# Row sums of attention over eight key blocks instead of four, with one add of each group on GpSimd

## The chip, the cores and the metric

The kernel runs on one core of one Trainium2 chip. The metric is the device time of one execution in microseconds (us); the median of several runs is given. The engines are TensorE (PE in the profile, its weight loads PEld), VectorE (DVE), ScalarE (ACT), GpSimd (POOL) and the queue of SyncE (SP).

## The reference, cut to what matters

The input is a batch of four images with 128 channels and 64 x 64 pixels. Layer 0 is group normalization, attention over the 4096 pixels of an image with four heads of 32 channels, an output projection and a residual. Layer 1 is two 3 x 3 convolutions with quantized weights, batch normalization, relu and a residual.

```python
x_norm = _group_norm(x, norm_w, norm_b)
qkv = jnp.einsum('oc,bchw->bohw', qkv_w, x_norm) + qkv_b[None, :, None, None]
q, k, v = jnp.split(qkv, 3, axis=1)
...
attn = jnp.einsum('bhid,bhjd->bhij', q, k) * scale
attn = jax.nn.softmax(attn, axis=-1)
out = jnp.einsum('bhij,bhjd->bhid', attn, v)
out = out.transpose(0, 1, 3, 2).reshape(b, c, h, w)
out = jnp.einsum('oc,bchw->bohw', proj_w, out) + proj_b[None, :, None, None]
return x + out
...
out = conv3x3_decomposed(x, lsq_quantize(w1, alpha1))
out = jax.nn.relu(batchnorm(out, gamma1, beta1))
out = conv3x3_decomposed(out, lsq_quantize(w2, alpha2))
out = batchnorm(out, gamma2, beta2)
out = jax.nn.relu(out + residual)
```

The change concerns the denominator of the softmax: for each head and query, the sum of the exponentials over all 4096 keys.

## The kernel before, in words

Attention is cut into 32 **blocks**: four images times eight groups of 512 queries. Each block goes through 32 **steps** (`kt`), one for each 128 keys. The keys lie on the partitions and the queries along the free dimension, so that the probabilities of one step are one tile `pt` of 128 partitions by four heads by 512 queries in float32 (128x2048). There are four such tiles (`bufs=4`).

A step consists of:

- `exp_step`: TensorE forms the scores of the four heads (L279) in two PSUM tiles `s` of two heads each, and ScalarE takes the exponential of each (L282). The pool of `s` has three tiles. The tiles of the projections and of the group norm's averages come from the same pool, in turn.
- `second`, which runs one step behind: `av_step` multiplies v with the probabilities and accumulates in `acc` (L289); `sum_step` adds probability tiles on VectorE (L302); `ones_step` (L306) multiplies the sum `r` with a matrix of ones on TensorE, which sums over the partitions and accumulates in `l`.
- `side_work`: the tasks of the block before, the quantization of the weights, the group norm of the next image (during the last but one block of an image) and its q, k and v projections (`project_qkv`, every fourth step of an image's last block, and of the very first block).

With `GROUPED = 4`, four steps share one product with ones: VectorE does three adds for four tiles. The product of a group is issued at the third step of the next group, behind `av_step`; that of a block's last group is a task of `finish`, `last_ones`, in the second step of the next block. The other tasks of `finish` follow, one per step: a copy of `l` to `ls` on ScalarE (L320), four reciprocals (L324), the running maxima `worst` and the product `at` (L327 to L329), an empty one, and `project`: the output projection `po` on TensorE (L333) and the residual add `xp` from PSUM on VectorE (L335).

Each engine works through its instructions in order. A scheduler sets that order from the order of the text and its own estimates. In the regular blocks it is that of the text but for small moves; in the first block the instructions of the weight quantization stand between others on VectorE. Semaphores follow from the tiles that an instruction reads and writes, and from the buffers that have to be free.

## Time and profile before

| | |
|---|---|
| median of 3 runs | 3028.28 us (3027.94 to 3031.02) |
| profiled execution | 3029.39 us, of it the span of the profile 3027.6 us |
| TensorE busy | 95% |
| VectorE busy | 73% |
| ScalarE busy | 69% |
| GpSimd busy | 1% |
| attention | ends at about 2699 us in the span, the convolutions follow |
| mean granted TensorE clock | 0.983 |

A line of the costliest groups reads: source line, engine, operation, tile written and tiles read, shapes of both (partitions x elements, type), count, then busy time and mean duration in ns, then the idle time of the engine just before these instructions and what ended most of it. A matrix product in float32 appears as two records. A line of the timeline reads: start in the span, duration, engine, line, operation, tiles, shapes, count of merged instructions, and in brackets the idle time before and what ended it. Busy time of TensorE counts pipelined products with modelled ends.

### The profile page before, as it was taken

Reading aid. Unit: us, or ns where it says so; the run is one execution under the profiler, and the core shown is the slowest. Engines: PE = TensorE matmul, PEld = TensorE weight load, DVE = VectorE, ACT = ScalarE, POOL = GpSimd, SP = SyncE. Lnnn points to the kernel's source line nnn. Section 1 sums busy time; section 2 is a strip of 40 time slices with the busy share of each in tenths; the row PEclk is TensorE's granted clock in tenths of the full one; section 3 lists DMA queues with packets and bytes.
Section 4 is the critical chain, followed back from the end, with each engine's and each line's share of the span. In section 5 each row is a group of like instructions: output and inputs, shape, how many; then the busy total and the mean of one; then the engine's idle time right before and its main releaser. Section 6 shows DMA issues by size and latency. Waiting matters only on the chain.

```text
span 3027.6 us, 45635 instructions
## 1 busy us (share of the span) xinstructions
PE 2884.3 (95%) x20050; PEld 928.2 (31%) x20050; DVE 2206.7 (73%) x1475; ACT 2100.7 (69%) x2209; POOL 18.5 (1%) x86
## 2 busy tenths in 40 slices
PE   5899999999999999999999999999999999989895
PEld 2222222223222222222222222232222222237773
DVE  8877777766777777767777777767777777763334
ACT  2488888856888888856888888757888888841223
POOL 1000000000000000000000000000000000000000
PEclk9899999999999999999999999999999999999997
DMA  6000000000000000000000000000000000000002
GB/s 124 9 1 1 1 1 1 1 1 1 1 1 1 1 1 1 1 1 1 1 1 1 1 1 1 1 1 1 1 1 1 1 1 1 1 1 1 1 0 113
DMA packets 36881, 21.30 MB, mean 7 GB/s; under 512 B 33777, under 2 KB 34545, under 8 KB 36673
## 3 DMA queue, kind: packets, MB, share of 16 engines
q1 hardware_dynamic: 32064, 16.91, 2.2%
q8 instruction: 159, 2.61, 0.4%
q10 hardware_dynamic: 4128, 1.05, 0.2%
q0 software_dynamic: 480, 0.33, 0.1%
q14 instruction: 50, 0.40, 0.0%
HBM read 9.90 MB, written 8.39 MB: 6 GB/s over the span
## 4 chain that ended last, share of the span: by engine, by line
PE 63%; DVE 28%; ACT 5%; issue 2%; DMA 1%; SPq 0%; DVEq 0%; POOL 0%; POOLq 0%; ACTq 0%
PE s L279 27%; PE acc L289 21%; DVE r L302 19%; PE ps L428 9%; PE l L306 5%; ACT p L282 5%; DVE rc L324 3%; DVE k L260 1%; DVE q L261 1%; DVE xp L335 1%; DVE at L329 1%; DVE worst L327 1%; DVE worst L328 1%; DMA out_dram<-y 0%; DVE st L222 0%
## 5 line engine op out<-in xcount | busy, mean ns | idle before, releaser
L282 ACT ACTIVATE p<-s 128x1024 f32<-128x1024 f32 x2048 | 1991.7, 1024 | 655.0 <-PE s L279 644.1
L279 PE MATMUL s<-q,k 32*128 32x512 f32 x8192 | 1293.6, 644 | 57.9 <-DVE q L261 47.0
L302 DVE TENSOR_TENSOR r<-r,p 128x2048 f32<-128x2048 f32 x512 | 1171.4, 2288 | 53.2 <-ACT p L282 9.2
L289 PE MATMUL acc<-p,v 128*32 128x512 f32 x8192 | 1100.9, 608 | 7.5 <-ACT av L313 7.5
L302 DVE TENSOR_TENSOR r<-p,p 128x2048 f32<-128x2048 f32 x256 | 586.7, 2292 | 541.8 <-ACT p L282 541.8
L279 PEld LDWEIGHTS s<-q,k 32*128 32x128 f32 x8192 | 411.5, 184 | 921.9 <-issue 548.5
L289 PEld LDWEIGHTS acc<-p,v 128*32 128x32 f32 x8192 | 162.1, 108 | 795.1 <-issue 761.7
L306 PE MATMUL l<-r,ones 128*32 128x512 f32 x2048 | 266.6, 592 | 1.8 <-DVE r L302 1.8
L459 ACT COPY cv<-ps 128x512 f32<-128x512 f32 x64 | 37.6, 588 | 208.3 <-PE ps L428 207.2
L428 PE MATMUL ps<-lo,wq 128*128 128x512 f32 x576 | 151.4, 408 | 11.6 <-DVE lo L419 11.6
L428 PE MATMUL ps<-hi,wq 128*128 128x512 f32 x576 | 148.4, 402 | 0.0
L428 PEld LDWEIGHTS ps<-lo,wq 128*128 128x128 f32 x576 | 110.4, 192 | 41.6 <-issue 12.1
L428 PEld LDWEIGHTS ps<-hi,wq 128*128 128x128 f32 x576 | 109.3, 190 | 29.4
L460 DVE BATCH_NORM_STATS2 st<-cv 128x6 f32<-128x512 f32 x64 | 44.3, 692 | 100.3 <-ACT cv L459 100.3
L306 PEld LDWEIGHTS l<-r,ones 128*32 128x32 f32 x2048 | 66.5, 110 | 155.3 <-issue 151.7
L324 DVE RECIPROCAL rc<-ls 128x128 f32<-128x128 f32 x128 | 108.2, 909 | 1.8 <-ACT ls L320 1.8
L478 ACT ACTIVATE t<-cv,bc,ba 128x1088 f32<-128x1088 f32 (+1 forms) x16 | 21.1, 1328 | 31.5 <-DVE lo L419 27.7
L418 DVE CAST hi<-t 128x1188 fp32r<-128x1188 f32 x16 | 12.5, 778 | 41.1 <-PE ps L428 39.7
L333 PE MATMUL po<-at,wp 128*128 128x512 f32 x64 | 36.9, 660 | 5.4 <-DVE at L329 5.4
L418 DVE CAST hi<-xp 128x1188 fp32r<-128x1188 f32 x16 | 12.3, 776 | 38.7 <-PE ps L428 38.7
L256 PE MATMUL pqk<-xn,wqkv 128*128 128x512 f32 x64 | 37.0, 660 | 3.0 <-DVE xn L253 3.0
L264 PEld LDWEIGHTS pv<-wqkv,xn 128*128 128x128 f32 x256 | 33.7, 192 | 15.6 <-issue 15.3
(98 smaller groups left out, 500.3 us busy)
## 6 DMA issues: line engine op xcount, KB each, us to landing
out_dram<-y SPq DMA_DIRECT2D x16, 512.0 KB, 2.7
xp<-in_x_dram SPq DMA_DIRECT2D x14, 512.0 KB, 7.7
wr<-in_L_conv_w_dram SPq DMA_DIRECT2D x6, 192.0 KB, 2.4
xp<-in_x_dram ACTq DMA_DIRECT2D x2, 512.0 KB, 10.5
wqkv<-in_L_conv_qkv_w_dram POOLq DMA_DIRECT2D x1, 192.0 KB, 6.6
bv<-in_L_conv_qkv_b_dram POOLq DMA_DIRECT2D x1, 64.0 KB, 7.2
wp<-in_L_conv_proj_w_dram POOLq DMA_DIRECT2D x1, 64.0 KB, 6.9
gamma<-in_L_conv_gamma_dram POOLq DMA_DIRECT2D x2, 0.5 KB, 6.5
```

What stands on the lines that cost most here:

```text
L256: nc.tensor.matmul(ps[:, 0, :], wqkv[:, P : 2 * P], xn, start=True, stop=True)
L264: nc.tensor.matmul(ps[:, 0, i * P : (i + 1) * P], xn[:, i * P : (i + 1) * P], wqkv[:, 2 * P : 3 * P], start=True, stop=True)
L279: nc.tensor.matmul(s[h // 2][:, h % 2, :], k[h * D : (h + 1) * D, c0 : c0 + P], q[h * D : (h + 1) * D, :], start=True, stop=True)
L282: nc.scalar.activation(pt[:, 2 * i : 2 * i + 2, :], s[i], AF.Exp, scale=SCALE)
L289: nc.tensor.matmul(acc[h * D : (h + 1) * D, :], v[:, kt % KB, h * D : (h + 1) * D], pt[:, h, :], start=(kt == 0), stop=(kt == NK - 1))
L302: nc.vector.tensor_tensor(r, pts[kt - 1] if n == 1 else r, pts[kt], ALU.add)
L306: nc.tensor.matmul(l[h * D : (h + 1) * D, :], ones, sums[g][:, h, :], start=(g == 0), stop=(g == NK // GROUPED - 1))
L324: nc.vector.reciprocal(rc[:, cs], ls[:, cs])
L333: nc.tensor.matmul(ps[:, 0, :], wp, at, start=True, stop=True)
L428: nc.tensor.matmul(ps, w[:, tap, :], part[:, j * RB + kh : j * RB + kh + RB, kw : kw + W], start=(n == 0), stop=(n == 2 * TAPS - 1))
L459: nc.scalar.copy(dst, ps)
L460: nc.vector.bn_stats(st[:, b * NB + j, :], dst)
```

## The change

`GROUPED` becomes 8, so that a block has four products with ones. The first two tiles of a group are added on GpSimd into a tile of their own, `rp` (one buffer). VectorE adds the third and fourth into `r` (one buffer instead of two), then one tile at each of the four following steps, and at the sixth step also `rp`.

```diff
-GROUPED = 4
+GROUPED = 8
...
         def sum_step(blk, kt, pts, sums):
-            n = kt % GROUPED
-            if n == 0:
-                return
+            n, g = kt % GROUPED, kt // GROUPED
             if n == 1:
-                sums[kt // GROUPED] = pex.tile([P, HEADS, FB], F32,
-                                               name=f"r_{blk[0]}_{blk[1]}_{kt}", tag="r")
-            r = sums[kt // GROUPED]
-            nc.vector.tensor_tensor(r, pts[kt - 1] if n == 1 else r, pts[kt], ALU.add)
+                sums["pool"] = pex.tile([P, HEADS, FB], F32, name=f"rp_{blk[0]}_{blk[1]}_{kt}",
+                                        tag="rp", bufs=1)
+                nc.gpsimd.tensor_tensor(sums["pool"], pts[kt - 1], pts[kt], ALU.add)
+            if n == 3:
+                sums[g] = pex.tile([P, HEADS, FB], F32, name=f"r_{blk[0]}_{blk[1]}_{kt}", tag="r",
+                                   bufs=1)
+                nc.vector.tensor_tensor(sums[g], pts[kt - 1], pts[kt], ALU.add)
+            if n > 3:
+                nc.vector.tensor_tensor(sums[g], sums[g], pts[kt], ALU.add)
+            if n == 5:
+                nc.vector.tensor_tensor(sums[g], sums[g], sums["pool"], ALU.add)
```

The condition in `second` that issues a product with ones (`kt % GROUPED == 2 and kt >= GROUPED`) is unchanged; with 8 it holds at steps 10, 18 and 26.

## The prediction

> **What bounds the kernel now.** I read the page's engine line and its chain, then the costliest groups, then the waits, then the timeline of a stretch without projections.

> ```profile
> PE 2884.3 (95%) x20050; PEld 928.2 (31%) x20050; DVE 2206.7 (73%) x1475; ACT 2100.7 (69%) x2209; POOL 18.5 (1%) x86
> PE 63%; DVE 28%; ACT 5%; issue 2%; DMA 1%; SPq 0%; DVEq 0%; POOL 0%; POOLq 0%; ACTq 0%
> L302 DVE TENSOR_TENSOR r<-r,p 128x2048 f32<-128x2048 f32 x512 | 1171.4, 2288 | 53.2 <-ACT p L282 9.2
> L302 DVE TENSOR_TENSOR r<-p,p 128x2048 f32<-128x2048 f32 x256 | 586.7, 2292 | 541.8 <-ACT p L282 541.8
> L306 PE MATMUL l<-r,ones 128*32 128x512 f32 x2048 | 266.6, 592 | 1.8 <-DVE r L302 1.8
> ```

> TensorE is nearly always busy, VectorE comes second, GpSimd is free. VectorE's idle time sits before the first add of each group (541.8 us, 2.1 us each); the ones products are 266.6 us in 256 calls, 1.04 us each. They wait for a sum 1.8 us in the whole run.

> ```profile
> 1528.03 2.29 DVE L302 TENSOR_TENSOR r<-p,p 128x2048 f32<-128x2048 f32 x1 [2.39 <-ACT p L282]
> ...
> 1529.19 1.25 PE L279 MATMUL s<-q,k 32*128 32x512 f32 x8
> ...
> 1530.37 1.94 ACT L282 ACTIVATE p<-s 128x1024 f32<-128x1024 f32 x2 [0.19 <-PE s L279]
> ...
> 1530.43 4.69 DVE L302 TENSOR_TENSOR r<-r,p 128x2048 f32<-128x2048 f32 x2
> ...
> 1531.26 1.04 PE L306 MATMUL l<-r,ones 128*32 128x512 f32 x8
> ...
> 1532.23 1.14 PE L279 MATMUL s<-q,k 32*128 32x512 f32 x8
> ...
> 1540.73 1.04 PE L306 MATMUL l<-r,ones 128*32 128x512 f32 x8
> ...
> 1581.98 1.13 PE L333 MATMUL po<-at,wp 128*128 128x512 f32 x2
> ...
> 1583.03 1.17 PE L279 MATMUL s<-q,k 32*128 32x512 f32 x8
> ...
> 1584.76 0.75 DVE L335 SCALAR_TENSOR_TENSOR xp<-po,bp,xp 128x512 f32<-128x512 f32 x1
> ...
> 1585.56 1.14 PE L279 MATMUL s<-q,k 32*128 32x512 f32 x8 [0.36 <-DVE xp L335]
> ```

> Four steps take 9.47 us (1531.26 to 1540.73). The step with ones takes 3.04 (1529.19 to 1532.23), the others 2.14 on average, so a ones call costs TensorE some 0.9 of its path. Below, S3 is the score products of the step with kt mod 8 = 3 (S33: the second step of the next block), p3 its probabilities, AV3 its product with v. p is complete 3.12 us after S starts (ScalarE's second exp ends at 1530.37 + 1.94 = 1532.31, S at 1529.19). Dependent adds start 2.40 apart. The last line is the weak spot: the projection po takes one of three score slots, and the scores two steps later wait until VectorE has emptied it. A whole block of 32 steps takes 77.43 us (previous projection at 1504.55).

> [...]

> **The change, part by part.**

> 1. *Ones products.* 128 of 256 calls go. Two groups of four take 2 x 9.47 = 18.94; one group of eight with one call would take 3.04 + 7 x 2.14 = 18.02. So 0.92 each, 3.7 us per block, 118 in all, on the path as long as TensorE sets the pace. The text emits them for a group of eight after AV of the next group's third step; the block's last call stays where it is, behind the next block's S1 and AV0.

> 2. *VectorE adds.* Six per eight steps before (3 + 3), six after (one p+p, four r+p, one r+rp): nothing saved. What changes is when: before, three start at the second step of each four; now all six start at the fourth step of eight and run back to back, 5 x 2.40 + 2.29 = 14.3 us. GpSimd's part replaces no VectorE add.

> 3. *GpSimd adds.* 128 new ones[...]. Nothing of importance is queued behind them there (a 1-element pow per image). Lower bound: they hide altogether beside other work; a gain below nothing is excluded, since VectorE keeps as many adds. Upper bound: VectorE stands still for each[...]. I take the upper one[...]. [...]

> 4. *Buffers.* r goes from two to one: the next group's first add waits for the ones call, which ends 3.04 after S3 starts, while p3 is there at 3.12: nothing, while TensorE isn't late. p0 and p1 now leave with the GpSimd add; exp of step 4 may wait up to 1.4 us for them, which ScalarE (1.94 of 2.14 per step) recovers slowly.

> Sum of an *inner group*, zero at S3. TensorE needs 18.0 (18.94 before). VectorE alone: adds at 3.2, 6.2 (p4), 8.6, 11.0, 13.4, 15.8, end 18.1: in time. With exclusion: p1 of the next group comes at 13.7 + 3.12 = 16.8, inside the last add; GpSimd starts at 18.1, ends 22.6, the next add starts there. The loop is 4.5 + 14.3 + 0.1 = 18.9: the gain of 0.9 is gone.

> Sum of a *block's seam*, zero at the end of the 32nd step's add. The last ones call would be due at S33 + 2.5 us, which is 16.2 in the clock of the last group, but the sum ends at 18.1: TensorE stalls about 1.9 (3.5 with exclusion). Then ones and S2 at 1.0; ls at 1.75; four reciprocals (3.38) to 5.2; worst, at, worst (0.6 each) to 7.1; six adds to 21.4; xr, in order behind them, to 22.2. TensorE reaches S8 at 13.8, po 15.9, S9 16.95; S10 is due at 19.1 and needs xr: 22.25, a stall of 3.1 against 0.36 before. S11 is at 24.3, its add at 27.5, that group's end at 42.4. Without exclusion S27 is at 60.3 and the last add ends 78.4; with it the last two groups end at 61.3 and 80.2. So a block takes 80.2 (78.4 without exclusion) against 77.43: +2.8 (+1.0).

> *Projection blocks* (one while the image changes, three times; the first block alike): k, q, v (0.75, 0.74, 0.68) stand behind the group's last add at every second projection; the scores' second slot waits for q. In the trace two first adds of a four-group lie 13.72 apart there (680.44 to 694.16), so eight steps take 27.5. After, zero at S3: first add to 6.9, k and q to 8.3, S4's second slot 8.35, S5 to S7 at 10.4, 12.5, 14.6, the second projection's products to 19.5; meanwhile the other five adds from p4 (10.6) on end at 23.1, q at 24.6, and only then S8's second slot, which was due at 20.6. S11 follows some 6.3 later; GpSimd, triggered late, is early for that group and gives 1 back: 30. So +2.5 x 4 = 10 per block, 30 for three, and 10 for the first, where weight quantization is mixed in as well. *Norms*, three: TensorE's two averaging products hold score slots until VectorE's copies, now behind an add burst: about one more add and a half, 3 each, 9. *Tail* of the last block: its last add ends some 3 later than now after the last exp.

> 28 x 2.8 + 30 + 10 + 9 + 3 = +130. The profiled execution took 3029.39 (span 3027.6 and 1.8 around it); it becomes 3159.4. The median of the runs is 1.1 lower, so 3158. Convolutions, DMAs and the SP queue are untouched.

> **Rivals.**
> - *GpSimd overtakes* (0.22). When VectorE lags over 1 us, GpSimd's request falls before the group's last add and takes its turn first; the sum, the ones call behind it and TensorE are late by 4.5. My clocks come within 0.5 us of this at the 32nd step (sixth add at 77.9, request at some 77.9 with exp held back, 77.4 without). For: nothing orders the two. Against: exp of that step is itself held back by the p buffers. One overtaking per block: 28 x (2.8 + 4.5) + 52 = +256, 3285.
> - *No exclusion* (0.18): GpSimd runs beside VectorE. For: the trace shows nothing against it. 28 x 1.0 + 24 (projections) + 5 + 6 + 3 = +66, 3094.
> - *TensorE-bound, faster* (0.09): xr and the last ones call do not hold TensorE, whose queue then only loses the 118 us: 2910 at best, some 2970 if half is given back. For: 95% busy TensorE. It decides where the seam's new stalls stay below 3.7 us a block; I count 1.9 + 2.7 = 4.6 even without exclusion, since six adds that start at p3 cannot end before S3 + 17.4, and xr comes after them.
> - *No difference* (0.06): stalls of about 3.7 per block, and projections that cost nothing.
> That the ones calls are not halved is excluded by the text: 32/8 groups per block.

> **How the numbers follow.** The likeliest, exclusion with GpSimd taking its turn after the sixth add, has 0.45: 3158, with 3110 to 3200 for the rough terms. Faster by over 0.2% (6 us, about what a measurement of this kernel can tell) 0.09, within 0.06, slower 0.85. The range, 3060 to 3290, leaves out the faster and equal cases and little of the others.

> **What would show.** After: the ones row at x1024 and about 133 us; 768 VectorE adds still; 128 GpSimd rows of about 4.5 us, and under exclusion no VectorE add beginning within one (or adds of 4 to 7 us, if a record includes the wait); TensorE waiting for xr some 3 us per block and for r at the last ones call 2 to 3.5; blocks of 80 us. Wrong, if blocks are under 77.4, or if inner groups take 18.0 and not 18.9.

## The result, and the profile after

The changed kernel takes 3193.66 us (median of four runs, 3188.78 to 3197.18) against 3028.22: a ratio of 1.0543, 95% interval 1.0525 to 1.0561. The profiled execution took 3188.78 us, its span 3187.1, TensorE's mean granted clock 0.950 (0.983 before). 159 us were lost between the two profiled executions, 165 between the medians; the prediction had 130.

From the page of the changed kernel: busy time by engine, then the chain that ended last. The chain's shares add up to 31% of the span (it was followed back over the last third only), so little is read from it.

```profile
PE 2896.3 (91%) x19026; PEld 913.8 (29%) x19026; DVE 2287.8 (72%) x1475; ACT 2095.7 (66%) x2209; POOL 693.5 (22%) x214
...
PE 21%; DVE 9%; ACT 1%; DMA 0%; issue 0%; DVEq 0%; POOL 0%; POOLq 0%; SPq 0%; ACTq 0%
```

TensorE does 1024 records fewer, yet its busy time rose by 12 us. That is the first sign that products became slower. The groups of the changed kernel, columns as before:

```profile
L279 PE MATMUL s<-q,k 32*128 32x512 f32 x8192 | 1362.2, 667 | 135.7 <-DVE q L261 72.6
L306 DVE TENSOR_TENSOR r<-r,p 128x2048 f32<-128x2048 f32 x512 | 1173.6, 2292 | 100.8 <-ACT p L282 54.4
L289 PE MATMUL acc<-p,v 128*32 128x512 f32 x8192 | 1135.4, 625 | 7.4 <-ACT av L319 7.4
L300 POOL TENSOR_TENSOR rp<-p,p 128x2048 f32<-128x2048 f32 x128 | 674.9, 5273 | 2092.1 <-ACT p L282 2092.1
...
L304 DVE TENSOR_TENSOR r<-p,p 128x2048 f32<-128x2048 f32 x128 | 354.7, 2771 | 468.4 <-PE l L312 239.0
...
L308 DVE TENSOR_TENSOR r<-r,rp 128x2048 f32<-128x2048 f32 x128 | 293.4, 2292 | 13.1
L312 PE MATMUL l<-r,ones 128*32 128x512 f32 x1024 | 144.1, 636 | 60.3 <-DVE r L306 60.3
```

VectorE still does 768 adds (512 + 128 + 128). The ones products halved in number. The GpSimd add takes 5273 ns on average, and the first VectorE add of a group, L304, 2771 instead of 2292: those two hold each other up. The adds that follow (L306, L308) keep 2292 ns. For the scores (L279) and `acc` (L289), as many products as before, the lines of the kernel before are:

```profile
L279 PE MATMUL s<-q,k 32*128 32x512 f32 x8192 | 1293.6, 644 | 57.9 <-DVE q L261 47.0
L289 PE MATMUL acc<-p,v 128*32 128x512 f32 x8192 | 1100.9, 608 | 7.5 <-ACT av L313 7.5
```

Together they take 103 us more after the change.

What TensorE and ScalarE wait for in the changed kernel (sum, times, longest, in us):

```profile
ACT p L282 <- POOL rp L300: 74.8, 52, 1.9
...
PE s L279 <- DVE xp L341: 62.5, 28, 3.2
PE l L312 <- DVE r L306: 60.3, 29, 4.7
```

The second was, in the kernel before:

```profile
PE s L279 <- DVE xp L335: 10.9, 28, 0.7
```

That is 0.39 each, now 2.23. The third was 1.8 in all and is now 2.08 each.

*An inner group*, timeline of the changed kernel:

```profile
1538.80 4.69 DVE L306 TENSOR_TENSOR r<-r,p 128x2048 f32<-128x2048 f32 x2
...
1542.39 5.49 POOL L300 TENSOR_TENSOR rp<-p,p 128x2048 f32<-128x2048 f32 x1 [16.94 <-ACT p L282]
...
1545.57 1.04 PE L312 MATMUL l<-r,ones 128*32 128x512 f32 x8
...
1546.73 3.30 DVE L304 TENSOR_TENSOR r<-p,p 128x2048 f32<-128x2048 f32 x1 [3.25 <-PE l L312]
...
1547.91 3.87 ACT L282 ACTIVATE p<-s 128x1024 f32<-128x1024 f32 x4 [1.30 <-POOL rp L300]
...
1557.33 4.69 DVE L306 TENSOR_TENSOR r<-r,p 128x2048 f32<-128x2048 f32 x2
...
1563.85 1.04 PE L312 MATMUL l<-r,ones 128*32 128x512 f32 x8
```

VectorE's last add runs to 1543.49. The GpSimd record begins before that and ends 4.39 us after it. L304 begins inside the GpSimd record and ends 2.15 us after that one: each waits inside its own record until the other is done, the exclusion that the prediction assumed. ScalarE's exponentials stand still for 1.30 us, because the `p` tiles that GpSimd reads aren't free. The group takes 18.28 us from one ones product to the next. VectorE's own round is a little longer, 18.53 us from the end of one last add (1543.49) to that of the next (1562.02), but the sum is still there some 2 us before its product is due.

*The seam between two blocks*, the same timeline:

```profile
1580.60 1.07 PE L312 MATMUL l<-r,ones 128*32 128x512 f32 x8 [2.01 <-DVE r L306]
...
1596.70 1.12 PE L339 MATMUL po<-at,wp 128*128 128x512 f32 x2
1596.98 4.69 DVE L306 TENSOR_TENSOR r<-r,p 128x2048 f32<-128x2048 f32 x2
...
1601.58 0.75 DVE L341 SCALAR_TENSOR_TENSOR xp<-po,bp,xp 128x512 f32<-128x512 f32 x1
...
1602.38 1.14 PE L279 MATMUL s<-q,k 32*128 32x512 f32 x8 [2.49 <-DVE xp L341]
1603.45 1.73 PE L289 MATMUL acc<-p,v 128*32 128x512 f32 x8
...
1605.11 2.09 PE L279 MATMUL s<-q,k 32*128 32x512 f32 x8
```

Both stalls that the prediction placed are there: the last ones product waits for the sum, and the scores wait for the residual add, which stands behind the burst of adds. What the prediction did not have comes next: the product with v takes 1.73 us (1.07 elsewhere) and the scores after it 2.09 (1.14). The same stretch in windows of 2 us shows it (columns: window, length, TensorE's busy time, instructions, granted clock, DMA share, GB/s):

```profile
1600.00:1602.00 2.00, 0.00 (x0) 1.00 0.00 0
1602.00:1604.00 2.00, 1.62 (x12) 0.93 0.00 0
1604.00:1606.00 2.00, 2.00 (x12) 0.50 0.00 0
1606.00:1608.00 2.00, 2.00 (x16) 0.72 0.00 0
```

TensorE stands idle (2.49 us before the scores at 1602.38), and then runs at half clock (0.50 from 1604 to 1606). That the one brings the other is tested below (`e11_hold`).

### The profile page after: what moved, and what is told of

Read it like the earlier page. It is cut to its first block, busy times and chain, and to the rows that moved or that the text cites. A ratio compares the mean times of both kernels' runs of the same rounds, so it can differ in the third digit from the quotient of the medians.

```text
span 3187.1 us, 44125 instructions
## 1 busy us (share of the span) xinstructions
PE 2896.3 (91%) x19026; PEld 913.8 (29%) x19026; DVE 2287.8 (72%) x1475; ACT 2095.7 (66%) x2209; POOL 693.5 (22%) x214
## 5 line engine op out<-in xcount | busy, mean ns | idle before, releaser
L282 ACT ACTIVATE p<-s 128x1024 f32<-128x1024 f32 x2048 | 1986.6, 1023 | 742.5 <-PE s L279 652.5
L279 PE MATMUL s<-q,k 32*128 32x512 f32 x8192 | 1362.2, 667 | 135.7 <-DVE q L261 72.6
L306 DVE TENSOR_TENSOR r<-r,p 128x2048 f32<-128x2048 f32 x512 | 1173.6, 2292 | 100.8 <-ACT p L282 54.4
L289 PE MATMUL acc<-p,v 128*32 128x512 f32 x8192 | 1135.4, 625 | 7.4 <-ACT av L319 7.4
L300 POOL TENSOR_TENSOR rp<-p,p 128x2048 f32<-128x2048 f32 x128 | 674.9, 5273 | 2092.1 <-ACT p L282 2092.1
L279 PEld LDWEIGHTS s<-q,k 32*128 32x128 f32 x8192 | 429.5, 190 | 1050.9 <-issue 582.6
L304 DVE TENSOR_TENSOR r<-p,p 128x2048 f32<-128x2048 f32 x128 | 354.7, 2771 | 468.4 <-PE l L312 239.0
L289 PEld LDWEIGHTS acc<-p,v 128*32 128x32 f32 x8192 | 164.2, 110 | 834.1 <-issue 799.9
L308 DVE TENSOR_TENSOR r<-r,rp 128x2048 f32<-128x2048 f32 x128 | 293.4, 2292 | 13.1
L312 PE MATMUL l<-r,ones 128*32 128x512 f32 x1024 | 144.1, 636 | 60.3 <-DVE r L306 60.3
L326 ACT COPY ls<-l 128x512 f32<-128x512 f32 x32 | 18.7, 585 | 82.7 <-PE l L312 82.7
L312 PEld LDWEIGHTS l<-r,ones 128*32 128x32 f32 x1024 | 30.4, 110 | 146.9 <-DVE r L306 86.6
L424 DVE CAST hi<-t 128x1188 fp32r<-128x1188 f32 x16 | 12.5, 779 | 41.1 <-PE ps L434 39.7
```

What stands on the lines that cost most here:

```text
L279: nc.tensor.matmul(s[h // 2][:, h % 2, :], k[h * D : (h + 1) * D, c0 : c0 + P], q[h * D : (h + 1) * D, :], start=True, stop=True)
L282: nc.scalar.activation(pt[:, 2 * i : 2 * i + 2, :], s[i], AF.Exp, scale=SCALE)
L289: nc.tensor.matmul(acc[h * D : (h + 1) * D, :], v[:, kt % KB, h * D : (h + 1) * D], pt[:, h, :], start=(kt == 0), stop=(kt == NK - 1))
L300: nc.gpsimd.tensor_tensor(sums["pool"], pts[kt - 1], pts[kt], ALU.add)
L304: nc.vector.tensor_tensor(sums[g], pts[kt - 1], pts[kt], ALU.add)
L306: nc.vector.tensor_tensor(sums[g], sums[g], pts[kt], ALU.add)
```

## The experiments

A block's length below is the distance between two `ls` copies, the mean of the 25 regular blocks without group norms or projections; "projection" is the range of the three blocks with the next image's projections. The "bank" of a tile is the place in PSUM that it takes. Before: 77.42 and 117.6 to 118.5; after: 80.84 and 130.7 to 133.6. Medians in us; ratios are to the kernel before, which took 3028.7 to 3030.4 beside them.

| run | what it is | median | ratio (95%) | block | projection |
|---|---|---|---|---|---|
| e1_vector8 | before, groups of eight | 3091.24 | 1.0206 (1.0189 to 1.0223) | 79.06 | 119.4 to 123.4 |
| e2_memset | after, memset for GpSimd's add | 3154.84 | 1.0417 (1.0400 to 1.0435) | 79.96 | 130.1 to 131.7 |
| e3_project | after, `project` two steps later | 3119.15 | 1.0302 (1.0285 to 1.0319) | 78.27 | 131.6 to 133.6 |
| e4_seam | after, all of `finish` two steps later | 3225.23 | 1.0647 (1.0629 to 1.0665) | 81.86 | 132.5 to 132.8 |
| e5_alternate | before, every other first add on GpSimd | 3059.61 | 1.0100 (1.0083 to 1.0117) | 77.20 | 129.1 to 130.0 |
| e6_vector8_project | e1 with e3's edit | 3062.81 | 1.0105 (1.0088 to 1.0122) | 78.24 | 119.3 to 122.0 |
| e7_memset_project | e2 with e3's edit | 3053.81 | 1.0077 (1.0060 to 1.0094) | 76.37 | 130.5 to 130.8 |
| e8_before_project | before with e3's edit | 3024.54 | 0.9983 (0.9976 to 0.9990) | 77.23 | 117.1 to 119.5 |
| e9_vector8_bank | e1, `po` in the bank of `l` | 2933.40 | 0.9682 (0.9666 to 0.9699) | 73.60 | 118.8 to 119.4 |
| e10_bank | after, `po` in the bank of `l` | 3109.96 | 1.0269 (1.0252 to 1.0287) | 78.00 | 131.0 to 133.7 |
| e11_hold | before, the scores held longer | 3149.26 | 1.0395 (1.0378 to 1.0412) | 81.42 | 118.8 to 120.8 |
| e12_bank_memset | e10 with e2's edit | 3057.28 | 1.0093 (1.0076 to 1.0110) | 76.36 | 129.1 to 132.0 |

### Groups of eight without GpSimd

```diff
-GROUPED = 4
+GROUPED = 8
```

> The kernel before with one part of the change alone: products with ones over eight key blocks, all seven adds of a group on VectorE, evenly spaced, r in two buffers as before, no GpSimd add. Theory (the loss comes from GpSimd's turn and from six adds packed into five steps; the halved products are a gain on TensorE's path): a group needs 18.0 us on TensorE and 7 x 2.40 = 16.8 on VectorE, both under 18.94; a block gains up to 3.7 us less what VectorE's finishing work (6 us per block) pushes out: 74 to 76 per regular block, 2920 to 2990 in all, and no exp waiting for a probability buffer for long. Rival (VectorE becomes the bound with seven adds): a block of 4 x 16.8 + 6 + 0.8 = 74 at least, but late sums stall TensorE as in the changed kernel: 77.4 or more, 3030 to 3100. Rival (the products with ones were hidden): 3028.

The theory missed. The timeline of this kernel, where the residual add is L335:

```profile
1543.16 0.75 DVE L335 SCALAR_TENSOR_TENSOR xp<-po,bp,xp 128x512 f32<-128x512 f32 x1
...
1543.96 1.14 PE L279 MATMUL s<-q,k 32*128 32x512 f32 x8 [3.69 <-DVE xp L335]
```

The last ones product has no wait here (seven adds that begin at a group's second step end in time), but the residual add stands behind five adds, and the scores wait 3.7 us per block for it. That is as much as the ones products save; slow products come on top (mean clock 0.960).

### GpSimd's part

```diff
-                nc.gpsimd.tensor_tensor(sums["pool"], pts[kt - 1], pts[kt], ALU.add)
+                nc.gpsimd.memset(sums["pool"], 1.0)
```

> The changed kernel with a GpSimd fill of rp in place of its add: GpSimd writes but reads no SBUF, does not wait for the probabilities and is done early. It leaves the first two tiles of each group out of the row sums. VectorE's adds, their order and the seam stay. Theory (exclusion costs about 1.8 us of a block's 3.5, the packed adds and the seam the rest): inner groups 18.0 us, blocks 78.4 plus what the lower clock after the two stalls takes, 78.4 to 79.5; first adds of a group back at 2.29 us, 3080 to 3130 in all. Rival (exclusion is the whole loss): 2910 to 2960. Rival (exclusion costs nothing): 3185 to 3200.

Taking away the GpSimd reads, and with them the exclusion and ScalarE's waits for the tiles that GpSimd reads, brings back 39 us of 165, less than expected; which of the two costs how much is not separated. L304 is back at 2291 ns. The cost of the reads is real and, taken away by itself, not the main loss.

### The projection later

```diff
-                    + [weigh, lambda: None, project])
+                    + [weigh] + [lambda: None] * 3 + [project])
```

> The changed kernel with the projection task two steps later (two empty tasks more), so that VectorE has its last add of the group behind it when po comes. Theory (the wait of the scores for xr, 2.2 us a block beyond TensorE's other waits and the slow products after it, is real but VectorE and GpSimd hold a loop of 18.9 a group): xr's wait goes to under 0.4 us; two to three us per block come back, 28 x 2.5 = 70: 3110 to 3140. Rival (only VectorE's and GpSimd's total counts): the wait moves to the next product with ones or to the probability buffers, 3170 to 3195.

75 us back, as expected: the wait for the residual add is gone. The last ones product still waits (65.2 us in all).

The control, the same edit on the kernel before:

> Control: the kernel before with only the projection two steps later. Theory (its scores wait 0.36 us a block for xr): 32 x 0.36 = 12 us come back at most, 3012 to 3030. Rival (the task's old place cost the kernel before as much as the changed one): 2950 or less.

6 us, as expected. The edit is worth something only where the burst made the residual add late.

The edit together with e1's groups of eight:

> Groups of eight with all seven adds on VectorE, as in the first experiment, and the projection task two steps later. Theory (in that experiment the only loss was the scores' wait for xr, 3.7 us a block, and the slow products of some 1.6 us after it): the wait goes, blocks are 73.7 to 75, under the 77.4 of the kernel before for the first time; 2930 to 2985 in all. Rival (VectorE's 74 us of work per block keep TensorE waiting anyway): the wait moves to the probability buffers or to the products with ones, 77 or more, 3030 to 3090.

Missed: the residual add moved two steps too and came to stand behind further adds, and the scores wait 2.6 us per block for it. A later place in the text doesn't free the bank earlier.

The edit together with the memset:

> The changed kernel with both GpSimd's reads taken away (a fill of rp in place of the add, which leaves two tiles of each group out of the sums) and the projection two steps later. Theory (the parts add up: exclusion 39 us, xr's wait 75 us): 3194 - 39 - 75 = 3080, 3065 to 3095; what is left against groups of eight on VectorE with the late projection is the wait for the block's last sum. Rival (both only relieve VectorE's one loop, and together give more than each): 3000 to 3060.

Together they bring 140 us, more than 39 + 75, as the second case had it. What is left is the wait for the last sum (53.4 us) and the projection blocks of 130.5 us.

### The whole seam later

```diff
-            return ([lambda: None, last_ones] + [lambda j=j: invert(j) for j in range(4)]
+            return ([lambda: None] * 3 + [last_ones] + [lambda j=j: invert(j) for j in range(4)]
```

> The changed kernel with the block's last product with ones, and all tasks behind it, two steps later, so that TensorE does not wait for the block's last sum. The four reciprocals and the maxima then fall between the six adds instead of into VectorE's gap. Theory (VectorE with GpSimd's turns is the loop): 4 x 18.9 + 5.3 = 81 per block, so no gain: 3170 to 3230, with the wait for the last sum gone (under 0.5 us a block) and a wait for the next group's sum in its place. Rival (the two seam stalls are the loss by themselves): both go, 78 per block, 3090 to 3120.

The total is as expected, the way to it is not. The reciprocals now fall into the burst and delay it, and GpSimd's next add then gets its turn before the group's last VectorE add: the prediction's rival of an overtaking GpSimd, here in 28 blocks, once in each. In those 28 cases L306 takes 6.3 to 6.4 us instead of 2.3. The groups of this kernel, then its waits:

```profile
L306 DVE TENSOR_TENSOR r<-r,p 128x2048 f32<-128x2048 f32 x512 | 1286.2, 2512 | 106.3 <-ACT p L282 67.2 <-DVE r L308 0.5
L300 POOL TENSOR_TENSOR rp<-p,p 128x2048 f32<-128x2048 f32 x128 | 716.0, 5594 | 2085.1 <-ACT p L282 1692.8 <-DVE r L308 392.3
...
ACT p L282 <- DVE r L306: 228.7, 78, 7.7
...
PE s L279 <- ACT p L282: 59.3, 28, 6.4
```

The wait that came in place of the one for the last sum (which fell from 60.3 to 24.1 us) is ScalarE's for these late adds, not the expected one for the next group's sum.

### GpSimd in every other group of four

```diff
-            nc.vector.tensor_tensor(r, pts[kt - 1] if n == 1 else r, pts[kt], ALU.add)
+            eng = nc.gpsimd if n == 1 and kt // GROUPED % 2 == 0 else nc.vector
+            eng.tensor_tensor(r, pts[kt - 1] if n == 1 else r, pts[kt], ALU.add)
```

> GpSimd alone: the kernel before with groups of four as they were, but the first add of every other group on GpSimd, straight into r. VectorE has five adds per eight steps left and GpSimd one, 128 in all as in the changed kernel. Theory (GpSimd's add blocks VectorE's adds, but costs only where VectorE has no slack): 5 x 2.40 + 4.5 = 16.5 us per eight steps against 18.94 on TensorE; the two engines take turns, GpSimd's rows are lengthened by waiting, blocks stay at 77.4 to 78 us, 3020 to 3050 in all. Rival (GpSimd's add by itself carries the loss, some 1.1 us a turn or more on TensorE's path): 3100 or more.

Regular blocks take 77.20, a little under the expected 77.4 to 78, and GpSimd's records are not lengthened: VectorE needs the partial sum from GpSimd before it goes on, so the two seldom ask at once, and the GpSimd add has its own length. Its group in this kernel:

```profile
L303 POOL TENSOR_TENSOR r<-p,p 128x2048 f32<-128x2048 f32 x128 | 582.9, 4554 | 2064.2 <-ACT p L282 2064.2
```

The total missed because the projection blocks grew by 11 to 12 us each, which the expectation had left out; why they grew so much was not looked into.

### The projection's product in another bank

The bank of `l` is free from the `ls` copy to the eleventh step of a block, and the residual add ends within that time. So the scores should never wait for it. The same edit (the residual add reads `ps` accordingly), which moves no instruction on any engine (the traces have the same order), was made on e1 and on the changed kernel:

```diff
-                ps = pss.tile([P, 2, FB], F32, name=f"po{b}_{qb}", tag="s")
-                nc.tensor.matmul(ps[:, 0, :], wp, at, start=True, stop=True)
+                ps = psa.tile([P, FB], F32, name=f"po{b}_{qb}", tag="l")
+                nc.tensor.matmul(ps, wp, at, start=True, stop=True)
```

> All seven adds of a group of eight on VectorE, and the projection's product goes into the PSUM bank of the row sums (free at that point) instead of one of the three banks that the scores rotate through. Theory (what groups of eight lost on VectorE alone is the scores' wait of 3.7 us per block for the residual add, plus products at half clock after it; what they save is 3.7 us of ones products per block): regular blocks 73.5 to 75.5 us against 78.9 with the same adds and the projection in a scores' bank, and 77.43 before; projection blocks 119 to 123; total 2950 to 2995 us, faster than the kernel before. Rival (the extra VectorE work per group delays the adds, so the exponentials' buffers come free late and the blocks stay long wherever the projection's product lies): blocks 77.5 to 79, total 3050 to 3090.

2933 us, a little below the expectation, and faster than both kernels. The residual add comes as late after `po` as in e1, 6.17 us (1605.62 to 1611.79 here, 1536.99 to 1543.16 there), and TensorE's products do not wait for it. From its page and its groups:

```profile
PE 2783.4 (95%) x19026; PEld 897.4 (31%) x19026; DVE 2496.4 (85%) x1603; ACT 2099.1 (72%) x2209; POOL 18.5 (1%) x86
...
L306 PE MATMUL l<-r,ones 128*32 128x512 f32 x1024 | 133.3, 592 | 2.0 <-DVE r L302 2.0
```

The ones products now take just half of their former 266.6 us, and a block is 3.82 us shorter than before: the 3.7 of the prediction's first part, without losses. VectorE does 896 adds instead of 768 and is 85% busy.

> The changed kernel with the projection's product in the PSUM bank of the row sums; no instruction moves on any engine. Theory (the scores' wait for the residual add, 2.2 us per block, and the half clock after it cost 2.5 to 3.5 us per block): blocks 77.3 to 78.5 against 80.9, total 3105 to 3135, as with the projection two steps later (3119). Rival (moving the projection two steps gained by taking the product past the burst of adds, not by freeing the scores' bank): blocks 79.5 to 81, total 3160 to 3195.

The gain is as expected: 84 us from freeing the bank alone. One thing in the reasoning did not hold: the half clock stayed (mean 0.955); it now follows the wait for the last sum, with products of 1.70 and 2.09 us where 1.04 and 1.14 are usual. Its timeline:

```profile
1614.70 1.70 PE L312 MATMUL l<-r,ones 128*32 128x512 f32 x8 [2.01 <-DVE r L306]
1616.33 2.09 PE L279 MATMUL s<-q,k 32*128 32x512 f32 x8
```

> The changed kernel with the projection's product in the bank of the row sums and, in place of the GpSimd add, a GpSimd memset of rp (p0 + p1 of each group are left out of the row sums): no exclusion and no wait for the residual add, only the six VectorE adds that start at the fourth step of a group. It is to be set beside 2933 us, where seven adds start at the second step and the projection lies in the same bank. Theory (most of the distance between 2933 and 3110 is the late start of the burst: the last ones products wait for it, 1.8 us per block, and projection blocks take 130): total 3040 to 3070, blocks 75.8 to 77, projection blocks 129 to 132, wait for the last sum 50 to 60 us in all. Rival (the distance is GpSimd's: exclusion and the waits for the p that it reads): total 2935 to 2980, blocks 73.6 to 74.5, projection blocks 119 to 122.

The theory held: 3057, with this wait still there although GpSimd reads nothing:

```profile
PE l L312 <- DVE r L306: 53.4, 29, 4.4
```

So the way from e9 to the changed kernel has three steps: 124 us for starting the adds at the fourth step of a group instead of the second (2933 to 3057), 53 for GpSimd's reads of `p` beside VectorE's adds (to 3110), and 84 for the projection in a scores' bank (to 3194). The sizes hold in this order only: the same reads cost 39 us between e2 and the changed kernel and 65 between e7 and e3. The first step also takes one of the two buffers from `r`; that is not its cost, since in e12, from the second block on, L304 never begins more than 0.62 us after the exponentials that it reads.

### The half clock by itself

```diff
+                for _ in range(4):
+                    nc.vector.tensor_copy(rc, ps[:, 0, :])
                 xr = rows(xp[b], qb * RB, RB)
```

> The kernel before with four redundant VectorE copies of the projection's product (0.6 to 0.75 us each) ahead of the residual add that frees its bank: 2.4 to 3.0 us more in which the scores wait, at the same place of each block, and nothing else changed. Theory (TensorE is granted half its clock for 3.4 or 6.8 us after an idle stretch of this length, which doubles the products that follow): blocks longer by the wait and 1.2 to 2 us more, 80.9 to 82.2 against 77.43, mean clock 0.955 to 0.97, total 3120 to 3175. Rival (the half clock is not brought by the wait): blocks longer by the wait alone, 79.5 to 80.5, mean clock 0.98, total 3090 to 3115. If the slack of later steps takes up part of the wait, both are lower by that part, and the clock still tells them apart.

The kernel before, with nothing added but four copies on VectorE (2.8 us) that hold the bank longer, loses 4.0 us per block, and its mean clock falls to 0.968 (0.981 for the kernel before beside it). Timeline of this kernel:

```profile
1571.20 1.16 PE L279 MATMUL s<-q,k 32*128 32x512 f32 x4 [1.86 <-DVE xp L337]
...
1572.29 1.94 PE L289 MATMUL acc<-p,v 128*32 128x512 f32 x8
...
1574.15 1.82 PE L279 MATMUL s<-q,k 32*128 32x512 f32 x8
```

The recorded wait is 1.75 us per block (54.4 in 31 waits), so 1.4 more than the 0.39 before. More than half of the rest is the half clock: 0.032 of 3151.8 us missing in the clock is 202 us at half speed, 99 more than before (103), so at most some 50 us or 1.6 per block. The remaining 1.0 us is not accounted for; the four products ahead of the wait have modelled ends (1.13 us for four, where eight take 1.14), so the true idle time may be longer than its record. Block, clock and total are as the theory said, and the rival, with its clock of 0.98, is out; the recorded wait was shorter than both had it.

## Why the prediction was right, and where its terms were off

The direction and the chain of waits are right. The price of one link, the inner group, is not, and a cost is missing; that the two errors lie on opposite sides is luck.

- **Ones products**: right, 0.92 us for each that goes. In e9 a block is 3.82 us shorter with four of them gone. In the changed kernel L312 took 144.1 us instead of 133, since some of them ran at half clock (1.44 us at 1661.19, shown at the end, instead of 1.04).
- **VectorE adds**: right, 768 as before, and the burst is there. That its late start is the largest of the three steps was in the sum but not named: it is the one from 2933 to 3057.
- **GpSimd adds, exclusion**: the exclusion, and 4.5 us for a GpSimd add, were the author's assumptions, with no trace behind them. That the adds of the two engines exclude each other is right, and the records show it as the prediction said they might, with the waiting inside them (GpSimd's up to 6.1 us, L304's up to 3.9); why they do is not shown. A GpSimd add by itself takes 4.55 us in e5. Reciprocals run beside a GpSimd add: at the seam above four of them take 3.39 us from 1582.35 on, partly inside GpSimd's record from 1579.40 to 1584.95, and 909 ns each on average, as before the change. What failed is the price in an inner group, 18.9 instead of 18.0: the two of a regular block take 18.14 and 18.29 us from one ones product to the next (18.14 each in e2), so the second of the prediction's signs of being wrong, groups of 18.0 and not 18.9, is all but met. Its loop of 18.9 is VectorE's, measured at 18.53, and within two groups it only uses up the time by which the sum was early. Of the 0.88 us that the reads cost a regular block (80.84 against 79.96 in e2), 0.66 lie between the third ones product and the last, the one that waits for its sum (16.77 against 16.11). In all the reads cost 39 to 65 us, where the two cases of the prediction lay 64 apart.
- **Seam**: both waits are where they were put, and both shorter: 2.08 instead of 3.5 for the last sum, 2.23 instead of 3.1 for the residual add. With the 3.7 saved this makes 2.23 - 0.39 + 2.08 - 3.7 = +0.2 per block, and a regular block grew by 3.42.
- **The missing term: products at half clock.** 0.050 of 3187.1 us missing in the clock is 319 us at half speed, against 103 before; with TensorE busy throughout, that is at most 108 us lost, 3.4 for each of 32 blocks. e11 shows the clock falling when nothing but a wait is added.
- **How 80.2 came close to 80.84**: the prediction's clock of VectorE can be set beside the trace. From the end of a block's last add, medians of the blocks without norms and projections, the first group ends at 22.1 (predicted 21.4), the next group's first add starts at 28.7 (27.5), and the other groups end at 43.5, 62.1 and 80.6 (42.4, 61.3, 80.2). It falls behind in the two places behind the waits, where slow products were seen, by 1.2 us together, and catches up 0.4 in each of the two inner groups. So the order of events is as predicted, and the nearness of the block is in part two errors that nearly cancel. TensorE, slowed, also came later to what it waits for, which fits the shorter waits; no run here separates that.
- **Projection and norm blocks**: right in kind, too small. Projection blocks grew by 12.2, 13.1 and 15.9 instead of 10, norm blocks by 8.9, 9.0 and 7.9 instead of 5.8. The q that the scores wait for behind the burst is in the waits (72.6 us, 47.0 before), and with adds that begin at the second step (e9) projection blocks stay at 119. The first `ls` comes 7.3 later instead of 10.
- **Rivals**: In the changed kernel GpSimd never overtook a group's last add: no record of L306 or L308 is over 2.3 us. It was no idle rival: e4, with the finishing work two steps later, has it in 28 blocks. "No exclusion" falls with e2. "TensorE-bound, faster" named 2910 and a point of decision, seam stalls below 3.7 us; the changed kernel doesn't reach it, and e9 does, at 2933. The argument against that rival, that six adds which start at the fourth step end too late whatever GpSimd does, is borne out by e12, which is slower than the kernel before with no GpSimd reads and no wait for the residual add.

## What to carry to other kernels

Before a wait is moved onto VectorE's queue, ask which PSUM bank the waiting result holds: a product that is not urgent belongs in a bank that the critical products don't rotate through, and the same edit was worth 84 (e10) and 158 us (e9) here once the queue had grown; on the kernel before, where that wait is 0.39 us, it was not run. When work is taken from TensorE, spread what replaces it: fewer VectorE instructions in a late burst cost more than one more of them that starts early. And price a stall of TensorE at more than its length, since products after it may run at half speed: in e11 a block with 1.4 us more of recorded wait became 4.0 us longer.

## What the runs showed of the hardware that was not expected

Where VectorE and GpSimd kept each other waiting, the wait stood inside the record of the one that waited and not as idle time before it: GpSimd's add takes 4.55 us in e5 and up to 6.1 in the changed kernel, a VectorE add 2.29 and up to 6.4 in e4.

```profile
1661.19 1.44 PE L312 MATMUL l<-r,ones 128*32 128x512 f32 x8 [2.01 <-DVE r L306]
1662.56 2.09 PE L279 MATMUL s<-q,k 32*128 32x512 f32 x8
```

Here the granted clock is 0.50 from 1661.75 to 1665.16. What decides between the two cases, and how long a wait has to be, does not come out of the records; no experiment sets the two apart.
